# A recurrent mixture-of-experts layer on one core: subtraction of halves from GpSimd to VectorE, code bits turned four tiles at a time, and setup rearranged

## The chip, the cores and the metric

The kernel runs on 1 core of one Trainium2 chip. The metric is the device time in microseconds. A core has five engines with queues of their own: PE (TensorE, matrix products), DVE (VectorE), ACT (ScalarE), POOL (GpSimd) and SP (SyncE, which here only issues DMAs). Each works through its instructions in order, and semaphores tie them together. Sixteen DMA engines move data between HBM and the on-chip memory SBUF; PE writes its products to another on-chip memory, PSUM.

## What is computed

The input x has 16 x 1024 = 16384 tokens of 512 numbers. Cut to what matters:

```python
xn = layernorm(x)                                   # over the 512
D = fractal_dimension(xn); filt = wave_filter(D, 512)
x1 = real(ifft(fft(xn) * filt))
bits = (sigmoid(x1 @ W_el + b_el) > 0.5)            # 24 bits per token
syn = (bits @ H.T > 0.5); w = syn.sum(-1)           # a 12-bit syndrome
corrected = flip the first 12 bits where syn, if 0 < w <= 3
s = x1 + corrected @ W_le + b_le
probs = softmax(xn @ router_w.T)                    # 8 experts, the best 2 are used
out = sum over the 2: (xn @ expert[e] + prob_e) * weight_e
return x + s * silu(out)
```

## The kernel before

A tile is 128 tokens, one per partition, so there are 128 tiles. Four make a block (one load of 1 MB), eight a group (GT), and sixteen a round of routing (RT).

**First pass** (`pass_1`, line 1053). The wave filter is folded, in setup, into small matrices cs, cd and cm, so that a tile needs these steps. `total` (line 431, DVE): pp, the sum of the two halves of x, and the sum over all 512. `level` (ACT): the mean. `spread` (line 451, ACT): the sum of squares. `scale`: from it the reciprocal deviation, for half a group or a group at once. `fold` (lines 490 to 495): sd, sum and difference of the quarters of pp, on DVE, and m (mm), the difference of the halves of x, on POOL. `transpose` (line 502, PE, then line 504 on ACT): both turned, into pmt. `filt` (lines 518 to 521, PE, then line 524 on ACT): the filtered tile and the logits, py, copied to yb. `store` (SP): yb to the array yd in HBM, a block at a time. `take_ex` (line 549, DVE): 24 code logits and 8 router logits.

The main loop, from line 1068, runs g over the tiles and writes each engine's order by hand (`manual_schedule`). `total` and `spread` run up to 12 and 11 tiles ahead, `fold` two ahead, `transpose` one ahead. Loads of x are issued 17 tiles ahead into five block buffers. The eight expert matrices of 1 MB each load at tiles 6, 10, ... 34. Besides, each iteration takes one step of the bit code (`code`: `bits`, two `turn_bits`, `syndrome`, `correct`), up to four of routing (`route`), some of the lists' arithmetic (`whole_ops`, in the queue `aside`), and one scatter. `None` in such a queue ends the iteration's share.

Routing finds each token's two experts, one of 28 pairs. It makes oh, 28 columns of which one is 1 for a token, ranks tokens within a pair by matrix products over a round (`rank`), and from that their places (dst). `scatter` (line 771, POOL) writes 12 bytes per token (mean, scale, number of the token) to that pair's list in HBM. A record rec of 32 numbers per token, with the weights, the bias and the corrected bits, goes to yd. Four record buffers are used in turn.

**Second pass** (line 1380). 101 "whole" tiles hold 128 tokens of the same pair: token rows, filtered rows and records are gathered by POOL (`fetch_x`, `fetch_y`, line 1135), x is normalized (line 1189, DVE), turned (`turn`, line 1196, PE; line 1198, ACT), and multiplied with both experts (`product`, line 1228, PE, four chunks by two passes for each expert). `turn_code`, `mend` and `spread_out` add the corrected code's share. `combine` and `put` finish the row. Remaining tokens go through 61 "item" tiles of one expert each, and 27 "rest" tiles that add up two parts. AHEAD_K, AHEAD_X, AHEAD_N and AHEAD_T say how many tiles ahead the list entry, x, the normalization and the turn are done. The last group's code and the last round's routing run in the first iterations of the second pass.

Of the kernel before, what the change touches and what calls it, by code (L numbers as in the profile page):

```python
# [27 lines left out]
def pairs_of(ne=8):  # L28

    return [(a, a + d) for d in range(1, ne) for a in range(ne - d)]  # L30
# [3 lines left out]
def kernel(  # L34
# [114 lines left out]
    ht_b = p1c.tile([L, 12], BF16, name="ht_b")  # L149
# [15 lines left out]
    ht = sp.tile([L, 12], F32, name="ht")  # L165
# [23 lines left out]
    def constants():  # L189
# [26 lines left out]
        kf = kf[:, 0:KC]  # L216
# [13 lines left out]
        v.memset(eps, EPS)  # L230

    def more_constants():
# [11 lines left out]
        for r in recs:  # L244
            g.memset(r, 0.0)
            g.memset(bits_of(r)[:, :, L : L + 1], 1.0)
        for py in pys:
            v.memset(py[:, 1, X + H : WY], 0.0)

    def setup():  # L250
# [19 lines left out]
        nc.tensor.matmul(pm[:, NS - 1 :], st.own, sums[:, NS - 1 :], start=True, stop=True)  # L270
        above = sp.tile([P, NS, HW], F32, name="above")
# [7 lines left out]
        nc.tensor.matmul(pn, st.all, cnt, start=True, stop=True)  # L279
        ly = sp.tile([P, NS], F32, name="ly")  # L280
        v.tensor_scalar(ly, pn, 1.0, None, ALU.max)
        nc.scalar.activation(ly, ly, AF.Ln)
# [19 lines left out]
        v.tensor_sub(wt[:, 2:4, :], lat[:, 0:2, :], lat[:, 2:4, :])  # L302
        gain = sp.tile([P, KC], F32, name="gain")
# [10 lines left out]
        for i in range(2):  # L314
            for c in range(2):
                nc.tensor.matmul(
                    pys[1][:, i, 0:H], bas[:, 2 + c, i * P : (i + 1) * P], gbas[:, 2 + c, :],
                    start=(c == 0), stop=(c == 1),
                )
        v.tensor_add(wt[:, 0, :], wp[:, 0, :], wp[:, 1, :])  # L320
        v.tensor_sub(wt[:, 1, :], wp[:, 0, :], wp[:, 1, :])
        for g in range(2):
            total(g)
            spread(g)
        nc.scalar.copy(cs[:, X:], pys[0][:, 0, 0:Q])
        nc.scalar.copy(cd[:, X:], pys[0][:, 1, 0:Q])
        for g in range(2, 4):
            total(g)
            spread(g)
        level()  # L330
        nc.scalar.copy(cm[:, :, X:], pys[1][:, :, 0:H])
# [3 lines left out]
        fold(0)  # L335
# [12 lines left out]
        for op in scale(0, slice(0, TPT)):  # L348
            op()
# [3 lines left out]
        for g in range(4, GT):  # L353
            total(g)
            spread(g)
        level()
# [65 lines left out]
    def total(g: int):  # L422

        k, j = groups[g // GT], g % GT
        if j == 0:
            k.sum = small.tile([P, GT], F32, name="sum")
            k.sq2 = small.tile([P, GT], F32, name="sq2")
            k.low = small.tile([P, GT], F32, name="low")
# [12 lines left out]
    def level():  # L441
        while means:
            k, js = means.pop()
            nc.scalar.activation(k.low[:, js], k.sum[:, js], AF.Copy, scale=-4.0 / E)
            nc.scalar.activation(k.rec[:, js, 10], k.sum[:, js], AF.Copy, scale=1.0 / E)
# [38 lines left out]
    def fold(g: int):  # L484
# [6 lines left out]
            sd[:, 0:Q], p[:, 0:Q], k.low[:, j : j + 1], p[:, Q:H], ALU.add, ALU.add  # L491
# [3 lines left out]
        nc.gpsimd.tensor_tensor(m, xr[:, 0:H], xr[:, H:E], ALU.subtract)  # L495
# [57 lines left out]
    def code(s: int):  # L553
# [3 lines left out]
        def bits():  # L557

            k.bits = bits_of(k.rec)[:, :, 0:L]
# [4 lines left out]
        def turn_bits(h):  # L564
            if h == 0:
                k.bt = small.tile([L, GT, P], BF16, name="bt", bufs=2)
            pg = ps_g.tile([P, 512], F32, name="pg")[0:L].rearrange("l (j t) -> l j t", t=P)
            for j in range(TPT):
                nc.tensor.matmul(
                    pg[:, j, :], k.bits[:, h + j, :], ident_b, start=True, stop=True  # L570
                )
            nc.scalar.copy(k.bt[:, h : h + TPT, :], pg)

        def syndrome():
            k.pg = ps_g.tile([P, 512], F32, name="pg")[:, 0 : GT * 12].rearrange(
                "p (j n) -> p j n", n=12
            )
            for j in range(GT):
                nc.tensor.matmul(k.pg[:, j, :], k.bt[:, j, :], ht_b, start=True, stop=True)

        def correct():
# [12 lines left out]
                k.bits[:, :, 0:12], k.bits[:, :, 0:12], fix, ALU.not_equal  # L594
# [20 lines left out]
    def route(n: int):  # L615
# [30 lines left out]
        def total():  # L646
            st.sm = new("sm", [P, S])
            v.tensor_reduce(st.sm, st.pb, AX.X, ALU.add)
# [32 lines left out]
        def chosen():  # L681
            st.sel = new("sel", SN, BF16)
            v.tensor_add(st.sel, st.hot1, st.hot2)
# [7 lines left out]
        def den_of():  # L691
            st.den = new("den", [P, S])
            v.tensor_add(st.den, st.sm, st.p2)

# [3 lines left out]
            lambda: v.reciprocal(st.sm, st.sm),  # L698
            lambda: v.tensor_mul(st.p2, st.p2, st.sm),
            den_of,  # L700
            lambda: v.tensor_scalar(st.den, st.den, 1e-6, None, ALU.add),
# [4 lines left out]
        def pair(d, at):  # L706
            if d == 1:
                st.oh = new("oh", [P, S, NPAIR], BF16)
            v.tensor_mul(
                st.oh[:, :, at : at + NE - d], st.sel[:, :, 0 : NE - d], st.sel[:, :, d:NE]  # L710
            )

        at = 0
        for d in range(1, NE):
            ops.append(lambda d=d, at=at: pair(d, at))
            at += NE - d
# [3 lines left out]
        def quads():  # L720
            st.q4 = small.tile([P, 4, NPAIR], BF16, name="q4", bufs=1)[:, 0:A]
            with nc.allow_low_precision("counts up to 4"):
                v.tensor_reduce(
                    st.q4, st.oh.rearrange("p (a b) k -> p a k b", b=4), AX.X, ALU.add
                )
# [60 lines left out]
        def weigh():  # L786
            st.w1 = new("w1", [P, S])
# [746 lines left out]
```

## Time and profile before

| | |
|---|---|
| median of 3 runs | 1370.36 us (1369.69 to 1370.8) |
| the profiled execution | 1371.99 us, its span 1370.0 us |
| PE busy | 1323.9 us (97%) |
| DVE busy | 927.1 us (68%) |
| POOL busy | 884.1 us (65%) |
| ACT busy | 602.7 us (44%) |
| first eviction of a filtered tile (line 524) starts | 27.7 us |
| last one starts | 326.3 us |
| line 495, POOL, 128x256 f32 | 128 times, mean 793 ns |
| line 771, POOL, a scatter of 128 entries | 128 times, mean 1067 ns |
| line 1228, PE | 2104 matrix instructions, busy 940.0 us |

The shares are means over two very different passes, so a row has to be read in its stretch of the time. [...] The ends of PE's instructions are modelled, so distances between starts say more than durations there. ACT and DVE also begin an instruction before the one ahead has ended.

### The profile page before, as it was taken

Reading aid. Unit: us, or ns where it says so; the run is one execution under the profiler, and the core shown is the slowest. Engines: PE = TensorE matmul, PEld = TensorE weight load, DVE = VectorE, ACT = ScalarE, POOL = GpSimd, SP = SyncE. Lnnn points to the kernel's source line nnn. Section 1 sums busy time; section 2 is a strip of 40 time slices with the busy share of each in tenths; the row PEclk is TensorE's granted clock in tenths of the full one; section 3 lists DMA queues with packets and bytes.
Section 4 is the critical chain, followed back from the end, with each engine's and each line's share of the span. In section 5 each row is a group of like instructions: output and inputs, shape, how many; then the busy total and the mean of one; then the engine's idle time right before and its main releaser. Section 6 shows DMA issues by size and latency. Waiting matters only on the chain.

```text
span 1370.0 us, 18162 instructions
## 1 busy us (share of the span) xinstructions
PE 1323.9 (97%) x4944; PEld 737.5 (54%) x4944; DVE 927.1 (68%) x2635; ACT 602.7 (44%) x1298; POOL 884.1 (65%) x879
## 2 busy tenths in 40 slices
PE   5999999989999999999999999999999999999996
PEld 4887777765444444444444444444444444444442
DVE  6898999974765788611111137787778877787775
ACT  6998999975322222222222223333333333333332
POOL 3367777876767554577554046777777777777741
PEclk9999999999999999999999999999999999999998
DMA  6998877836333432355446244555555555655531
GB/s 216 353 319 283 254 243 238 256 108 201 85 104 107 141 109 76 112 170 168 138 141 190 75 134 136 181 173 179 174 172 183 179 176 175 187 173 175 181 121 39
DMA packets 119216, 233.75 MB, mean 171 GB/s; under 512 B 37356, under 2 KB 71020, under 8 KB 115023
## 3 DMA queue, kind: packets, MB, share of 16 engines
q0 software_dynamic: 47264, 135.54, 32.8%
q1 hardware_dynamic: 71386, 96.88, 21.2%
q8 instruction: 43, 0.70, 0.2%
q14 instruction: 55, 0.44, 0.1%
q10 hardware_dynamic: 468, 0.19, 0.1%
HBM read 144.79 MB, written 87.75 MB: 170 GB/s over the span
## 4 chain that ended last, share of the span: by engine, by line
PE 82%; DVE 7%; issue 4%; ACT 2%; POOL 2%; DMA 1%; POOLq 0%; DVEq 0%; SPq 0%; ACTq 0%
PE pe L1228 62%; PE py L521 5%; PE pt L1196 5%; PE pt L502 3%; PE py L518 2%; PE py L519 2%; PE pg L1261 1%; DVE pp L431 1%; DVE sd L490 1%; POOL out L1312 1%; DMA yd<-yb 1%; ACT no L451 1%; DVE sd L493 1%; ACT yb L524 1%; PE pc L1249 1%
## 5 line engine op out<-in xcount | busy, mean ns | idle before, releaser
L1228 PE MATMUL pe<-w_sb,xt 128*128 x2104 | 940.0, 594 | 1.2 <-issue 1.2
L1228 PEld LDWEIGHTS pe<-w_sb,xt 128*128 128x128 f32 x2104 | 394.9, 190 | 417.3 <-issue 411.6
L1279 ACT ACTIVATE acc<-acc,yg 128x512 f32<-128x512 f32 x128 | 92.4, 722 | 406.8 <-DVE acc L1278 406.8
L1278 DVE SCALAR_TENSOR_TENSOR acc<-pe,yg,acc 128x512 f32<-128x512 f32 x101 | 75.7, 749 | 180.2 <-PE pe L1228 180.0
L1198 ACT COPY xt<-pt 128x512 f32<-128x512 f32 x162 | 93.6, 578 | 171.7 <-PE pt L1196 171.7
L1312 POOL DMA_INDIRECT out<-xg,toks x101 | 112.3, 1112 | 82.0 <-DVE xg L1307 55.5
L771 POOL DMA_INDIRECT lists<-rec,dst x128 | 136.6, 1067 | 33.9 <-issue 22.4
L495 POOL TENSOR_TENSOR mm<-xt 128x256 f32<-128x256 f32 x128 | 101.5, 793 | 82.4 <-PE pt L502 63.5
L1189 DVE TENSOR_SCALAR xn<-xg,entry 128x512 f32<-128x512 f32 x61 | 34.8, 571 | 173.4 <-PE pt L1196 170.1
L521 PE MATMUL py<-cm,pmt 128*128 128x288 f32 x512 | 147.2, 411 | 0.0
L1135 POOL DMA_INDIRECT yg<-yd,toks x101 | 107.2, 1061 | 61.6 <-ACT acc L1279 29.6
L1135 POOL DMA_INDIRECT xg<-in_x,toks x101 | 108.6, 1075 | 40.7 <-issue 27.5
L1275 ACT ACTIVATE acc<-pe,yg 128x512 f32<-128x512 f32 x101 | 68.9, 682 | 135.0 <-PE pe L1228 102.4
L1196 PEld LDWEIGHTS pt<-ident,xn 128*128 128x128 f32 x648 | 81.0, 141 | 86.6 <-issue 84.3
L524 ACT ACTIVATE yb<-py,rec 128x640 f32<-128x640 f32 x128 | 101.5, 793 | 26.8 <-PE py L521 23.0
L1135 POOL DMA_INDIRECT xg<-in_x,entry x88 | 89.9, 1021 | 29.6 <-issue 25.9
L1135 POOL DMA_INDIRECT part<-ed,adr_r x54 | 65.7, 1217 | 65.0 <-DMA ed<-res 48.8
L521 PEld LDWEIGHTS py<-cm,pmt 128*128 128x128 f32 x512 | 91.9, 193 | 13.9
L1196 PE MATMUL pt<-ident,xn 128*128 128x128 f32 x648 | 97.3, 273 | 1.6 <-DVE xn L1189 0.8
L1307 DVE TENSOR_TENSOR xg<-mix,xg 128x512 f32<-128x512 f32 x128 | 88.5, 692 | 4.4
L451 ACT ACTIVATE no<-xt,sum 128x512 bf16<-128x512 f32 x128 | 91.0, 711 | 1.2 <-DVE pp L431 1.2
L1135 POOL DMA_INDIRECT entry<-lists,adr_i x61 | 62.9, 1032 | 41.7 <-DVE xn L1189 24.7
(270 smaller groups left out, 1766.1 us busy)
## 6 DMA issues: line engine op xcount, KB each, us to landing
xt<-in_x SPq DMA_DIRECT2D x32, 1024.0 KB
yd<-yb SPq DMA_DIRECT2D x32, 576.0 KB
yd<-yb SPq DMA_DIRECT2D x32, 512.0 KB
ed<-res SPq DMA_DIRECT2D x61, 256.0 KB
w_sb<-in_expert_w SPq DMA_DIRECT2D x8, 1024.0 KB
yd<-rec SPq DMA_DIRECT2D x36, 64.0 KB
lists<-rec,dst POOLq DMA_INDIRECT x128
xg<-in_x,toks POOLq DMA_INDIRECT x101
```

What stands on the lines that cost most here:

```text
L451: nc.scalar.activation(no, xts[g // TPT][:, g % TPT, :], AF.Square, bias=k.sum[:, j : j + 1], scale=-float(E), accum_out=k.sq2[:, j : j + 1],)
L495: nc.gpsimd.tensor_tensor(m, xr[:, 0:H], xr[:, H:E], ALU.subtract)
L521: nc.tensor.matmul(py[:, 1, 0 : X + H], pmt[:, 2 + c, :], cm[:, c, :], start=(c == 0), stop=(c == 1))
L524: nc.scalar.activation(y_room(g), py[:, :, 0:WY], AF.Copy, scale=k.rec[:, j, 11:12])
L771: dma = nc.gpsimd.indirect_dma_start(out=lists, out_offset=bass.IndirectOffsetOnAxis(ap=st.dst[:, j : j + 1], axis=0), in_=st.rec.bitcast( ...
L1135: nc.gpsimd.indirect_dma_start(out=dst, out_offset=None, in_=src, in_offset=bass.IndirectOffsetOnAxis(ap=idx, axis=0), bounds_check=limit - 1,
L1196: nc.tensor.transpose(pt[:, c * P : (c + 1) * P], k.xn[:, c * P : (c + 1) * P], ident)
L1198: nc.scalar.copy(k.xt.rearrange("p c t -> p (c t)"), pt)
L1228: nc.tensor.matmul(pe.unsqueeze(1), k.xt[:, c, :], w_sb[:, bass.ds(e, 1), c, :], start=(c == 0), stop=(c == KC - 1),)
L1279: nc.scalar.activation(k.acc, k.acc, AF.Silu, bias=k.rec[:, 9:10])
L1307: nc.vector.tensor_add(k.x, k.mix, k.x)
L1312: dma = nc.gpsimd.indirect_dma_start(out=of, out_offset=bass.IndirectOffsetOnAxis(ap=k.tok, axis=0), in_=k.x, in_offset=None, bounds_check ...
```

## The change

1. **m by VectorE.** In `fold` the difference of the halves is made by DVE. POOL has only DMA work in the pass.
2. **One mean.** `level` writes -4/512 of the sum into the record and nothing else; `fold` reads it there. Who needs the mean in the second pass multiplies by -0.25.
3. **Bits of four tiles.** The 24 bits of four tiles, now in a tile of their own, are turned by one product (96 rows), and the syndrome of four tiles comes from one product with a block-diagonal matrix. Twelve of the bits are copied to the record by ACT.
4. **Routing.** The pairs are ordered by cyclic distance, so that four products make all 28 columns; sel has 12 columns. Sums of four tiles are two additions. The two chances (probabilities) lie side by side in one tile, so that weights and biases take one operation each.
5. **Setup.** The clearing of records and of PSUM moves from POOL and from the beginning to DVE and into the setup's waits; the arguments of the filter are made behind the first products; the first tiles' sums, folds and turns are placed among the setup's steps; fewer squares (`spread`) stand ahead of the first filtered tile.
6. **The passage and the second pass.** List entry, x, normalization and turn go one tile further ahead. Turns of items use another PSUM pool; `turn_code` has four slots in one bank; `whole_ops` starts with a None, and one None more stands behind it.

The diff, cut:

```diff
 def pairs_of(ne=8):
-    return [(a, a + d) for d in range(1, ne) for a in range(ne - d)]
+    near = [(a, (a + d) % ne) for d in range(1, ne // 2) for a in range(ne)]
+    return [tuple(sorted(k)) for k in near] + [(a, a + ne // 2) for a in range(ne // 2)]
...
         for i, x_ in enumerate(lx):
             v.memset(st.slope[:, i : i + 1], -(n * x_ - sum(lx)) / den)
-        kf = kf[:, 0:KC]
+        v.memset(eps, EPS)
+        st.kf = kf[:, 0:KC]
+
+    def arguments():
+        v, kf = nc.vector, st.kf
         kr = sp.tile([P, KC], F32, name="kr")
...
-        for r in recs:
-            g.memset(r, 0.0)
-            g.memset(bits_of(r)[:, :, L : L + 1], 1.0)
-        for py in pys:
-            v.memset(py[:, 1, X + H : WY], 0.0)
+
+    def clear(r):
+        nc.vector.memset(r, 0.0)
+        nc.vector.memset(bits_of(r)[:, :, L : L + 1], 1.0)
...
         nc.tensor.matmul(pm[:, NS - 1 :], st.own, sums[:, NS - 1 :], start=True, stop=True)
+        arguments()
...
         nc.tensor.matmul(pn, st.all, cnt, start=True, stop=True)
+        clear(recs[0])
...
+        total(0)
         gain = sp.tile([P, KC], F32, name="gain")
...
+        for g in range(1, 4):
+            total(g)
         v.tensor_add(wt[:, 0, :], wp[:, 0, :], wp[:, 1, :])
         v.tensor_sub(wt[:, 1, :], wp[:, 0, :], wp[:, 1, :])
-        for g in range(2):
-            total(g)
-            spread(g)
+        spread(0)
+        level()
+        fold(0)
+        spread(1)
...
+        spread(3)
+        fold(1)
+        begin, middle, end = scale(0, slice(0, TPT))
+        begin()
         nc.scalar.copy(cs[:, 0:L], pw[:, 0, :])
         nc.scalar.copy(cd[:, 0:L], pw[:, 1, :])
         nc.scalar.copy(cm[:, :, 0:L], pw[:, 2:4, :])
-        for g in range(4, GT):
-            total(g)
-            spread(g)
-        level()
+        middle()
+        transpose(1)
+        end()
+        total(4)
+        spread(4)
+        clear(recs[1])
+        total(5)
+        spread(5)
...
-            nc.scalar.activation(k.low[:, js], k.sum[:, js], AF.Copy, scale=-4.0 / E)
-            nc.scalar.activation(k.rec[:, js, 10], k.sum[:, js], AF.Copy, scale=1.0 / E)
+            nc.scalar.activation(k.rec[:, js, 10], k.sum[:, js], AF.Copy, scale=-4.0 / E)
...
-        nc.gpsimd.tensor_tensor(m, xr[:, 0:H], xr[:, H:E], ALU.subtract)
+        nc.vector.tensor_sub(m, xr[:, 0:H], xr[:, H:E])
...
-            pg = ps_g.tile([P, 512], F32, name="pg")[0:L].rearrange("l (j t) -> l j t", t=P)
-            for j in range(TPT):
+            pg = ps_g.tile([P, 512], F32, name="pg")[0 : TPT * L, 0:P]
+            nc.tensor.matmul(
+                pg, k.bits[:, h : h + TPT, :].rearrange("p j l -> p (j l)"), ident_b, start=True, stop=True
+            )
+            nc.scalar.copy(k.bt[:, h // TPT, :], pg)
+
+        def syndrome():
+            pg = ps_g.tile([P, 512], F32, name="pg")[:, 0 : GT * 12]
+            k.pg = pg.rearrange("p (j n) -> p j n", n=12)
+            nc.scalar.copy(bits_of(k.rec)[:, :, 12:L], k.bits[:, :, 12:L])
+            for h in range(GT // TPT):
                 nc.tensor.matmul(
-                    pg[:, j, :], k.bits[:, h + j, :], ident_b, start=True, stop=True
+                    pg[:, h * TPT * 12 : (h + 1) * TPT * 12], k.bt[:, h, :], ht_b,
+                    start=True, stop=True,
                 )
...
-            st.sel = new("sel", SN, BF16)
-            v.tensor_add(st.sel, st.hot1, st.hot2)
+            st.sel = new("sel", [P, S, NE + NE // 2], BF16)
+            v.tensor_add(st.sel[:, :, 0:NE], st.hot1, st.hot2)
+            v.tensor_copy(st.sel[:, :, NE:], st.sel[:, :, 0 : NE // 2])
...
-        for d in range(1, NE):
-            ops.append(lambda d=d, at=at: pair(d, at))
-            at += NE - d
+        for d in range(1, NE // 2 + 1):
+            ops.append(lambda d=d: pair(d, (d - 1) * NE))
...
-                v.tensor_reduce(
-                    st.q4, st.oh.rearrange("p (a b) k -> p a k b", b=4), AX.X, ALU.add
-                )
+            v.tensor_add(two, o4[:, :, 0:2, :], o4[:, :, 2:4, :])
+            v.tensor_add(st.q4, two[:, :, 0, :], two[:, :, 1, :])
...
-        aside.extend([lengths, None, full, None, rows_, None, where, upto, None, bounded])
+        aside.extend([None, lengths, None, full, None, rows_, None, where, upto, None, bounded])
...
-            while spreads and spreads[0] <= g + AHEAD_S and spreads[0] <= 2 * g + GT + 4:
+            while spreads and spreads[0] <= g + AHEAD_S and spreads[0] <= 2 * g + GT - 1:
...
-    AHEAD_K, AHEAD_X, AHEAD_P, AHEAD_Y, AHEAD_N, AHEAD_T = 9, 6, 4, 5, 4, 2
+    AHEAD_K, AHEAD_X, AHEAD_P, AHEAD_Y, AHEAD_N, AHEAD_T = 10, 7, 4, 5, 5, 3
...
+    pcs = ps_c.tile([96, 4, P], F32, name="pc")
...
+        if k.kind == "item":
+            k.mean = w2.tile([P, 1], F32, name="mean1", bufs=2)
+            nc.vector.tensor_scalar(k.mean, k.low, -0.25, None, ALU.mult)
...
-        pc = ps_c.tile([96, P], F32, name="pc")
+        pc = pcs[:, k.at % 4, :]
...
+        "turn": [max(k - AHEAD_T, min(k - 2, 3)) for k in range(NTILE)],
```

## The prediction

> **What bounds the kernel now.** I first cut the span into stretches at the starts of the evictions yb<-py (line 524, one for each of the 128 tiles of the first pass). Columns: stretch, length, busy us and count of PE, PEld, DVE, ACT and POOL, granted clock, DMA share, GB/s.
>
> ```profile
> 27.70:109.00 81.30, 81.19 (x521) 65.61 (x519) 73.92 (x266) 77.14 (x185) 41.25 (x48) 1.00 0.94 320
> 109.00:120.10 11.10, 8.78 (x44) 7.04 (x45) 8.55 (x32) 8.70 (x23) 5.41 (x7) 0.85 0.97 352
> 120.10:156.10 36.00, 35.98 (x235) 28.79 (x234) 32.38 (x121) 34.73 (x84) 28.96 (x33) 1.00 0.81 250
> 156.10:194.00 37.90, 36.34 (x235) 28.89 (x234) 37.08 (x130) 35.21 (x85) 29.23 (x33) 1.00 0.75 237
> 400.00:1361.00 961.00, 957.74 (x2865) 466.53 (x2863) 597.28 (x1439) 293.22 (x575) 619.79 (x568) 1.00 0.48 149
> ```
>
> Three regimes. From 27.7 to 120 (tiles 0 to 40) the DMA engines are 94 to 97% busy, because the eight expert matrices load beside the tiles. From 120 to 326 each round of 16 tiles takes 36.0 to 43 us. From 400 PE is never idle, so the second pass can lose only what stalls at its beginning. The change can win in the start, in the five and a half rounds after 120, and in the passage at 326 to 400.
>
> Next I read the timelines inside one round: PE, then ACT.
>
> ```profile
> 121.83 0.38 PE L502 MATMUL pt<-ident,sd 128*128 128x128 f32 x2
> ...
> 123.87 0.39 PE L569 MATMUL pg<-ident_b,rec 128*24 128x128 bf16 x4
> 124.20 0.44 PE L502 MATMUL pt<-ident,sd 128*128 128x128 f32 x2
> ```
>
> ```profile
> 122.03 0.79 ACT L524 ACTIVATE yb<-py,rec 128x640 f32<-128x640 f32 x1
> ...
> 123.98 0.79 ACT L524 ACTIVATE yb<-py,rec 128x640 f32<-128x640 f32 x1
> 124.67 0.56 ACT L572 CAST bt<-pg 24x512 bf16<-24x512 f32 x1
> 125.14 0.72 ACT L451 ACTIVATE no<-xt,sum 128x512 bf16<-128x512 f32 x1
> ```
>
> A plain tile takes 1.95 us (122.03 to 123.98). PE's instructions start back to back for all of it, and so do ACT's three (starts 0.69, 0.71 and 0.55 apart): the two are tied. A tile with turn_bits takes 2.43, and the tie holds: PE adds 0.48, ACT's cast 0.47. The round at 120.1 is 16 x 1.95 = 31.2 plus 4.8 for bits, syndrome, logarithms, means and rank.
>
> The third engine, DVE, is the slowest in the later rounds (37.08 of 37.90). The timelines of POOL and DVE side by side say why:
>
> ```profile
> 122.59 0.88 POOL L495 TENSOR_TENSOR mm<-xt 128x256 f32<-128x256 f32 x1
> 123.63 0.99 POOL L771 DMA_INDIRECT lists<-rec,dst  x1 [0.16 <-issue]
> ```
>
> ```profile
> 122.34 0.34 DVE L490 SCALAR_TENSOR_TENSOR sd<-pp,low 128x128 f32<-128x128 f32 x1
> 122.60 0.28 DVE L493 TENSOR_TENSOR sd<-pp 128x128 f32<-128x128 f32 x1
> 122.81 0.95 DVE L431 SCALAR_TENSOR_TENSOR pp<-xt 128x256 f32<-128x256 f32 x1
> ```
>
> Line 431 takes 0.41 elsewhere and 0.95 beside POOL's subtraction. Over the pass, line 493 averages 503 ns where it meets line 495, 280 where it meets only a scatter, and 281 where POOL is idle. Durations above the shortest of their form, at DVE instructions that meet line 495, add up to 9.6 us in the round from tile 64. So POOL's subtraction costs DVE about 0.5 us a tile, and the scatters cost it nothing.
>
> **m moves from POOL to DVE.** The row for a 128x256 f32 operation from SBUF on DVE is in the second pass:
>
> ```profile
> 389.54 0.42 DVE L1271 TENSOR_TENSOR mix<-mix,yg 128x256 f32<-128x256 f32 x1
> ```
>
> It lasts 0.42, but independent instructions start sooner: line 431, as wide, lets its follower start 0.34 after it. I charge 0.34 (ends 0.33 and 0.46): 16 x 0.34 = 5.4 a round. [...] DVE in the worst round: busy 36.6, less 9.6 stretch, plus 5.4 (by the rule 6.8) = 32.4 (33.8).
>
> [...]
>
> **Fewer DVE instructions in routing.** Seven products of line 709 (0.19 to 0.35 each, 1.8 in all) become four of about 0.29, near line 683's 0.28: -0.6. The reduction of line 723 (0.93) becomes two additions of about 0.28: -0.4. Den's two (0.31 and 0.43) become one; weigh and biases lose one each: -0.7. The copied half of sel adds 0.2. Ends overlap, so I take -1.2 of these 1.5. DVE: 31.2 a round, below what follows.
>
> **Bits of four tiles at once.** PE: four products of line 569, 56 ns apart, become one: -0.17, four times a round. Eight of line 579 (0.28 in the chain) become two: -0.2, twice. PE: -1.1 a round. ACT: the cast of 512 columns becomes one of 128. The row with that shape, ct<-pc (line 1253), lasts 0.26, so about 0.16 of issue in place of 0.47: -1.2 a round. One mean copy of two goes: -0.4. The new copy of 12 bits per tile adds 0.13 to 0.25, twice: +0.4. ACT: -1.2. As the two are tied, only the smaller counts: 36.0 - 1.1 = 34.9 a round, so DVE's 31.2 leaves PE and ACT as the bound.
>
> Rounds: at 120.1, 36.0 to 34.9: 1.1. At 156, 37.9: 3.0. At 194, 36.9: 2.0. At 231, 37.7; this one carries the whole-list arithmetic on DVE too, so I take 35.3: 2.4. The last eight tiles: 0.6.
>
> **The stall at tile 108.** The round at 268.6 takes 43.1. POOL holds the gather tt<-lists (276.85) for its scatters to land, and m queues behind it for 3.7; then DVE waits 1.9 for tt at line 906. With m on DVE the first wait reaches no tile. The second stays and may grow to 4, since DVE gets there sooner. I take 38.5: 4.6.
>
> **Setup.** DVE reaches line 263 at 5.81 without waiting. It was held by ten operations of the arguments (3.23 to 5.71), stretched to 0.4 to 0.7 by POOL's clears. Moved behind the first products, they fill idle 1.1 between 6.27 and 7.37 and overrun it by some 0.4; the clears now on DVE (0.55 and 0.17 on POOL) fall into gaps of 0.7. The chain starts 1.9 sooner, 1.5 after the overrun. Tiles 1's fold and turn come forward too, and ACT's idle 0.7, 0.5 and 0.2 between 16.7 and 23 closes in part. Five squares (0.71 each) go behind the first eviction; it comes 6 sooner, but ACT repays 3.5 in tiles 0 to 4. Net 3.2 (ends 1.5 and 4.5). The clears of records 2 and 3 at tile 4 lie beside 1.0 of DVE idle.
>
> **Tiles 8 to 40: nothing.** The DMA engines bind. All that is issued there is the same (25 MB at 350 GB/s, my count from the issues, is 71 us). It starts with tile 6, so it is shifted by the start's 3.2 and not shortened. Faster tiles wait longer at tile 36 (now 11.7 us in the chain for yd<-yb). If that cover goes, another 2 are won.
>
> **Passage to the second pass.**
>
> ```profile
> PE pg L853 <- DVE cum L814: 2.6, 1, 2.6
> PE pe L1228 <- issue: 1.2, 1, 1.2
> ```
>
> The one None ahead of lengths puts line 853 an iteration behind cum: 2.6 gone. The granted clock was 0.5 for 3.4 us after this pause; eight products took 5.4 instead of 3.4, so 2.0 more. Next late there is scatter and gather on POOL, with no PE wait behind it. Four slots for pc save one of two round trips to ACT in three iterations, 0.3 each; the mends still wait for ct: 0.7. The seventh xg and tenth entry go ahead on POOL, 1.07 each; the first yg waits 5.2 for yd anyway, so 0 (worst +1). The turn one tile earlier and the second bank change no PE work; the added scale of the mean, one small DVE operation in 61 items and one in each kept, lies in stretches with DVE 13 to 20% busy: 0. Sum 5.2.
>
> **Sum.** 3.2 + 1.1 + 3.0 + 2.0 + 2.4 + 4.6 + 0.6 + 5.2 = 22.1. The profiled execution took 1371.99 (span 1370.0), 1.6 above the median of 1370.36; the saving is carried over: 1370.4 - 22.1 = **1348**.
>
> **The rivals.** (a) *Ties hold.* PE's and ACT's extras fall on different tiles, and DVE at 90% waits in order, so rounds stay near 36: the first five terms after the start fall to 0, 1.9, 0.9, 1.5, 3.5: sum 16.2, 1354. For it: the round now is 0.9 above PE's own sum. (b) *DMA binds on.* Share 0.75 to 0.81 would rise with the pace; if yb's two buffers then wait for stores, only start and passage remain: 8.4, 1362. Against: 40 tiles after the experts it fell to 250 GB/s from 352. (c) *Slower: DVE becomes the bound.* If the stretch is not POOL's subtraction but comes with any POOL work, DVE keeps it: 36.6 + 5.4 - 1.2 = 40.8 a round, against a mean of 38. It decides from about 38 a round on. 5.5 rounds lose some 16, less 8.4: 1378. Against it are the 280 against 281 ns. (d) The new setup order starves ACT and the start loses what the rest wins: 1370.
>
> **How the numbers follow.** Forecast 0.50, (a) 0.25, (b) 0.15, (c) 0.07, (d) 0.03. The forecast's own range is 1340 to 1354: setup 1.5 to 4.5, the tt wait 2 to 7, DMA relief. Taking in (a) and (b) gives 1338 to 1364; (c) stays out. 0.2% is 2.7 us, about what a measurement here can tell from no change. Faster 0.90, within 0.03, slower 0.07.
>
> **What would show it.** Right: line 493's successor rows at 0.28 throughout; no POOL row but DMA in the pass; rounds at 34 to 35.5 with PE and ACT full; first yb near 22; no PE wait on cum. Wrong: DVE rows still stretched; DVE over 36 in a round; tile 36 no earlier; a new half-clock stretch at the passage.

## The result and the profile after

The changed kernel takes 1347.45 us, median of 4 runs (1346.75 to 1347.89); the kernel before, beside it, 1370.03 (1368.02 to 1370.80). The ratio is 0.9832, with an interval of 0.9820 to 0.9844: **22.6 us faster**, where 22.1 were forecast. The sum came out almost right; several of its terms did not. The span of the profiled execution is 1346.1 us against 1370.0, so 23.9 us are to be found between the two traces.

The head of the page of the changed kernel, to be held against the table of before:

```profile
span 1346.1 us, 17641 instructions
...
PE 1306.1 (97%) x4752; PEld 732.5 (54%) x4752; DVE 909.7 (68%) x2802; ACT 589.1 (44%) x1282; POOL 769.1 (57%) x743
```

PE is 97% busy in both. DVE's busy time even fell, by 17 us, though it took over 128 subtractions: what it no longer spends stretched, and the shorter routing, outweigh them. POOL is 115 us less busy. None of this says where the end moved, so the pass is cut as before, at starts of yb<-py (now line 535). Columns: stretch, length, busy us and count of PE, PEld (PE's weight loads), DVE, ACT and POOL, granted clock (PE's clock as a share of full speed, so 0.5 is half clock), DMA share (busy share of the 16 DMA engines), GB/s.

```profile
21.30:104.00 82.70, 77.49 (x458) 63.92 (x456) 70.23 (x299) 77.19 (x193) 17.31 (x16) 0.98 0.91 303
104.00:119.20 15.20, 9.55 (x47) 7.33 (x48) 11.41 (x55) 8.61 (x22) 0.00 (x0) 0.78 0.83 297
119.20:153.70 34.50, 34.13 (x212) 28.41 (x211) 30.80 (x137) 33.30 (x84) 16.58 (x16) 1.00 0.93 261
153.70:188.40 34.70, 34.05 (x212) 28.32 (x211) 32.05 (x141) 33.22 (x84) 16.98 (x16) 1.00 0.95 257
258.40:292.15 33.75, 33.75 (x214) 28.42 (x212) 31.39 (x138) 30.48 (x75) 19.12 (x16) 1.00 0.59 175
```

Three things are to be seen. The rounds from 119.2 on are 34 to 35 us, with PE and ACT full and DVE at 31 to 32: the picture that was forecast. The round with the former stall (the last line) is a plain round now. But the first 40 tiles end at 119.2, though the first eviction comes 6.4 earlier than before: in the second line PE works 9.55 of 15.20 us, at a granted clock of 0.78.

The starts of yb<-py, from both traces, give the balance. The first row's 3.2 is counted at tile 8, behind the squares that ACT has to make up.

| stretch | before us | after us | won | forecast |
|---|---|---|---|---|
| to tile 8 | 43.9 | 40.7 | 3.2 | 3.2 |
| tiles 8 to 40 | 76.2 | 78.6 | -2.4 | 0 |
| round 40 to 56 | 36.0 | 34.4 | 1.6 | 1.1 |
| round 56 to 72 | 37.9 | 34.7 | 3.2 | 3.0 |
| round 72 to 88 | 36.9 | 34.2 | 2.7 | 2.0 |
| round 88 to 104 | 37.7 | 35.8 | 1.9 | 2.4 |
| round 104 to 120 (the stall) | 43.1 | 33.8 | 9.3 | 4.6 |
| last eight tiles | 14.6 | 13.4 | 1.2 | 0.6 |
| from the last eviction to the end | 1043.7 | 1040.5 | 3.2 | 5.2 |

**DVE.** Its costliest groups from 115 to 260 us in the changed kernel: line, names, shapes and count, then busy us and mean ns of one.

```profile
L443 DVE SCALAR_TENSOR_TENSOR pp<-xt 128x256 f32<-128x256 f32 x66 | 27.7, 420 | 0.0
L506 DVE TENSOR_TENSOR mm<-xt 128x256 f32<-128x256 f32 x66 | 27.6, 418 | 0.0
...
L504 DVE TENSOR_TENSOR sd<-pp 128x128 f32<-128x128 f32 x67 | 19.1, 286 | 0.0
```

The same lines in the kernel before, from 150 to 275 us:

```profile
L431 DVE SCALAR_TENSOR_TENSOR pp<-xt 128x256 f32<-128x256 f32 x54 | 25.4, 470 | 0.0
L493 DVE TENSOR_TENSOR sd<-pp 128x128 f32<-128x128 f32 x54 | 19.4, 360 | 0.0
```

The subtraction (line 506) lasts 418 ns, as long as the second pass's row of that width in the trace of before (0.42 us); line 504, the old line 493, is at 286 on average, where it was 360 over all its instances there, 503 over those beside POOL's subtraction. POOL's scatters still run, and stretch nothing: over the whole first pass line 504 is at 286 in the 58 instances that meet a scatter, at 284 in the 70 others.

**The wait at tile 36.** ACT's timeline, the eviction of that tile; in brackets is the idle time before it, and what ended it:

```profile
108.30 0.79 ACT L535 ACTIVATE yb<-py,rec 128x640 f32<-128x640 f32 x1 [6.65 <-DMA yd<-yb]
```

The buffer yb is still being stored. The chain of work that ended last says how long the store of tiles 28 to 31, whose buffer tile 36 needs, held it up: start and length, first before, then now.

```profile
97.19 11.71 DMA yd<-yb
```

```profile
93.38 14.81 DMA yd<-yb
```

From tile 35 to tile 36 it is now 8.9 us, before 5.3, and the granted clock is 0.5 for 6.8 us from 106.8, before for 3.4 from 112.6. This is where the -2.4 of the table sits.

**The pause for tt.** POOL's timeline, then DVE's one line that reads the gathered tt:

```profile
248.06 0.97 POOL L787 DMA_INDIRECT lists<-rec,dst  x1 [0.30 <-issue]
256.62 1.25 POOL L907 DMA_INDIRECT tt<-lists,idx  x1 [7.58 <-DVE sd L504]
262.81 3.07 POOL L787 DMA_INDIRECT lists<-rec,dst  x1 [4.94 <-DVE woff L905]
```

```profile
264.90 0.32 DVE L918 COPY ttf<-tt 30x256 f32<-30x256 f32 x1
```

The same two in the kernel before:

```profile
276.85 1.06 POOL L895 DMA_INDIRECT tt<-lists,idx  x1 [3.74 <-DVE ex L549]
```

```profile
281.23 0.32 DVE L906 COPY ttf<-tt 30x256 f32<-30x256 f32 x1 [1.88 <-DMA tt<-lists,idx]
```

POOL has finished a round's scatters by 249, tt is issued at 256.62, 1.7 us ahead of the eviction of tile 104, and DVE reaches it 8.3 us later. Before, it was issued 8.3 us behind that eviction (268.56), and read 4.4 later. There is no idle time before line 918: DVE's wait for tt went wholly, not in part.

**The passage.** PE's instructions that waited for an engine's result, in three stretches from 305 to 347 us:

```profile
307.32 0.66 PE L1222 MATMUL pt<-ident,xn 128*128 128x128 f32 x4 [1.77 <-DVE xn L1211]
308.70 1.11 PE L1222 MATMUL pt<-ident,xn 128*128 128x128 f32 x4 [0.72 <-ACT xt L1224]
...
334.97 0.22 PE L1275 MATMUL pc<-ident_b,b 128*96 128x128 bf16 x1 [0.92 <-ACT ct L1279]
345.51 0.66 PE L1222 MATMUL pt<-ident,xn 128*128 128x128 f32 x4 [0.86 <-ACT xt L1224]
347.00 0.22 PE L1275 MATMUL pc<-ident_b,b 128*96 128x128 bf16 x1 [0.78 <-ACT ct L1279]
```

The wait for cum (2.6) is gone, with the half-clock stretch behind it. But the second pc product still waits for ACT's ct, as it did before by the same 0.92, though it now writes another slot: the slots saved nothing. Two turns fall into one iteration and wait for ACT's copy, a wait of 0.86 that was not there. And a half-clock stretch at 308 lasts 6.8 us, where the one at 331 in the trace of before lasted 3.4. So the time at half clock behind the last eviction is 6.8 in both traces (before 3.4 at 331 and 3.4 behind cum). Of the 3.2 won there, 1.5 is PE's idle time (21.0 to 19.4) and 1.7 its busy time, with twelve instructions fewer.

### The profile page after: what moved, and what is told of

Read it like the earlier page. It is cut to its first block, busy times and chain, and to the rows that moved or that the text cites. A ratio compares the mean times of both kernels' runs of the same rounds, so it can differ in the third digit from the quotient of the medians.

```text
span 1346.1 us, 17641 instructions
## 1 busy us (share of the span) xinstructions
PE 1306.1 (97%) x4752; PEld 732.5 (54%) x4752; DVE 909.7 (68%) x2802; ACT 589.1 (44%) x1282; POOL 769.1 (57%) x743
## 4 chain that ended last, share of the span: by engine, by line
PE 84%; ACT 5%; issue 4%; DMA 3%; POOL 1%; DVE 1%; POOLq 0%; SPq 0%; ACTq 0%; DVEq 0%
PE pe L1254 63%; PE py L532 6%; PE pt L1222 3%; DMA yd<-yb 3%; PE pt L513 3%; PE py L529 2%; PE pg L1222 2%; ACT no L462 2%; PE py L530 2%; PE pg L1287 1%; ACT yb L535 1%; ACT pmt L515 1%; POOL out L1338 1%; PE pc L1275 1%; DMA xt<-in_x 0%
## 5 line engine op out<-in xcount | busy, mean ns | idle before, releaser
L1338 POOL DMA_INDIRECT out<-xg,toks x101 | 108.6, 1075 | 82.9 <-DVE xg L1333 56.7
L1211 DVE TENSOR_SCALAR xn<-xg,mean,entry 128x512 f32<-128x512 f32 x61 | 34.7, 569 | 166.7 <-PE pg L1222 166.3
L1224 ACT COPY xt<-pg 128x512 f32<-128x512 f32 x56 | 32.8, 586 | 156.7 <-PE pg L1222 156.7
L1154 POOL DMA_INDIRECT part<-ed,adr_r x54 | 62.8, 1163 | 64.9 <-DMA ed<-res 48.8
L1332 DVE TENSOR_TENSOR mix<-mix,acc 128x512 f32<-128x512 f32 x128 | 87.6, 685 | 0.8 <-ACT acc L1305 0.8
L1222 PEld LDWEIGHTS pt<-ident,xn 128*128 128x128 f32 x424 | 53.2, 142 | 58.5 <-issue 51.1
L515 ACT COPY pmt<-pt 128x512 f32<-128x512 f32 x128 | 73.7, 576 | 1.8 <-PE pt L513 1.6
```

Source lines behind the costliest of these rows:

```text
L515: nc.scalar.copy(pmts[g], pt)
L1154: nc.gpsimd.indirect_dma_start(out=dst, out_offset=None, in_=src, in_offset=bass.IndirectOffsetOnAxis(ap=idx, axis=0), bounds_check=limit - 1,
L1222: nc.tensor.transpose(pt[:, c * P : (c + 1) * P], k.xn[:, c * P : (c + 1) * P], ident)
L1332: nc.vector.tensor_mul(k.mix, k.mix, k.acc)
L1338: dma = nc.gpsimd.indirect_dma_start(out=of, out_offset=bass.IndirectOffsetOnAxis(ap=k.tok, axis=0), in_=k.x, in_offset=None, bounds_check ...
```

## The experiments

The runs met chips of two kinds. Most fell on chips where the kernel before takes 1370 to 1372 us, as above. On two others it takes 1444.2 and 1458.5 us, and there the parts of the change behave differently; apart from the run on the bits, the runs of those chips are told last. The theory under test is the prediction's: POOL's subtraction stretches DVE, and once it is gone PE and ACT set the pace.

### The subtraction back on POOL, all else changed

```diff
-        nc.vector.tensor_sub(m, xr[:, 0:H], xr[:, H:E])
+        nc.gpsimd.tensor_tensor(m, xr[:, 0:H], xr[:, H:E], ALU.subtract)
```

> The changed kernel with m back on POOL once more, since the first time the kernel before itself took 1444. If the chip gives before near 1370 again: theory (POOL's subtraction stretches DVE and ties POOL to the loop) 1360 to 1365 with rounds after tile 40 at 36 to 37 and the tt wait back; rival (the stretch only fills idle DVE) 1347 to 1351. If before is near 1444 again: about 1428 as the first time.

Measured: 1369.97 us (1366.15 to 1371.64) beside 1371.97, ratio 0.9984 (0.9974 to 0.9994). That is above the 1360 to 1365 expected: everything else together is worth 2 us without this one line. The groups of DVE from 130 to 260 us:

```profile
L443 DVE SCALAR_TENSOR_TENSOR pp<-xt 128x256 f32<-128x256 f32 x54 | 26.0, 481 | 0.0
L504 DVE TENSOR_TENSOR sd<-pp 128x128 f32<-128x128 f32 x53 | 25.4, 480 | 0.0
```

and one round of it, in the columns of the stretches above:

```profile
152.80:190.90 38.10, 35.21 (x211) 28.10 (x209) 37.14 (x124) 34.00 (x83) 29.62 (x32) 1.00 0.81 236
```

Line 504 is back at 480 ns, with fewer DVE instructions than before, and the round is DVE's: 37.14 busy of 38.10. Three rounds (56 to 104) take 38.1, 38.1 and 38.8, where 36 to 37 were expected, and the round with tt 45.1. So PE's and ACT's savings had nothing to win.

### The kernel before with only the subtraction moved

```diff
-        nc.gpsimd.tensor_tensor(m, xr[:, 0:H], xr[:, H:E], ALU.subtract)
+        nc.vector.tensor_sub(m, xr[:, 0:H], xr[:, H:E])
```

> The kernel before with m on DVE alone, once more. On a chip that gives before near 1371: theory (m's move carries nearly all of the gain, since with m on POOL the other parts gave 2 us): -12 to -17, so 1354 to 1359, rounds after tile 40 at 36.0 to 36.5 (PE and ACT tied, bits as before), no pause at tile 108. Rival (DVE needs the shorter routing as well: 32.4 a round is not enough slack in order): rounds at 37 and more, -3 to -8. Rival (m's move is worth nothing without the new setup and bits): within 3 us of before.

Measured: 1365.74 us (1363.79 to 1368.62) beside 1370.46, ratio 0.9969 (0.9958 to 0.9979): 4.7 faster, where more than twice that was expected. Groups of DVE from 130 to 260 us, then two rounds:

```profile
L495 DVE TENSOR_TENSOR mm<-xt 128x256 f32<-128x256 f32 x57 | 23.8, 417 | 0.0
...
L493 DVE TENSOR_TENSOR sd<-pp 128x128 f32<-128x128 f32 x57 | 16.3, 286 | 0.0
```

```profile
120.30:156.33 36.03, 36.02 (x235) 28.83 (x234) 31.85 (x137) 34.76 (x85) 16.38 (x16) 1.00 0.88 258
156.33:192.36 36.03, 36.02 (x235) 28.82 (x234) 33.05 (x144) 34.76 (x85) 17.05 (x16) 1.00 0.91 248
```

In the pass the theory held: DVE is unstretched, and the plain rounds are 36.03 and 36.03, PE busy 36.02, with the old bits. The pause for tt is gone here too. From the first to the last eviction 9.7 us are won (298.6 to 288.9). The passage and second pass gave 1.4 back (1045.1), and the profiled execution was the fastest of the eight, 1.9 below their median. So the size for the whole kernel was missed, the mechanism was not.

The two runs together: one part alone is worth 4.7, all the others alone 2.0, both 22.6. Two bounds lay close above each other, DVE at 37 to 38 a round and PE with ACT at 36; lifting either shows the other.

### Bits turned one tile at a time

```diff
-            pg = ps_g.tile([P, 512], F32, name="pg")[0 : TPT * L, 0:P]
-            nc.tensor.matmul(
-                pg, k.bits[:, h : h + TPT, :].rearrange("p j l -> p (j l)"), ident_b, start=True, stop=True
-            )
+            pg = ps_g.tile([P, 512], F32, name="pg")[0:L].rearrange("l (j t) -> l j t", t=P)
+            for j in range(TPT):
+                nc.tensor.matmul(
+                    pg[:, j, :], k.bits[:, h + j, :], ident_b, start=True, stop=True
+                )
...
-            for h in range(GT // TPT):
+            for j in range(GT):
                 nc.tensor.matmul(
...
+                    k.pg[:, j, :], k.bt[:, j, :], ht_b[0:L, 0:12], start=True, stop=True
                 )
```

> The changed kernel with the bits turned, and the syndromes made, tile by tile as before, all else as changed. Theory (PE and ACT are tied once DVE is free, so each turn costs 0.4 to 0.5 a tile again): rounds after tile 40 longer by 1.1 to 1.6 (a tile with a turn 2.43 and 2.5 in place of 2.02 and 2.11), 5.4 rounds, +6 to +8, so 1353 to 1356. Rival (another engine binds, the turns are covered): rounds within 0.4, +0 to +2.

This ran on the chip where the kernel before takes 1458.5, beside the changed kernel without the None ahead of lengths (told below): 1546.96 (ratio 1.0657, 1.0575 to 1.0740) against 1530.66. Both stall there behind tile 27, so the 16 us between them are not used. Tiles 8 to 24 are undisturbed in both: 35.7 us against 34.2, so the bits are worth 1.5 us a round, within the 1.1 to 1.6 expected. What that makes of the whole kernel on the other chips was not measured. PE's timeline says where, first with bits one by one, then four at once:

```profile
43.70 0.39 PE L581 MATMUL pg<-ident_b,bits 128*24 128x128 bf16 x4
44.03 0.44 PE L513 MATMUL pt<-ident,sd 128*128 128x128 f32 x2
```

```profile
44.64 0.22 PE L580 MATMUL pg<-ident_b,bits 128*96 128x128 bf16 x1
44.69 0.39 PE L513 MATMUL pt<-ident,sd 128*128 128x128 f32 x2
```

From the first turn of bits to PE's next instruction it is 0.33 us, then 0.05: 0.28 saved, four times a round. The same reading of the syndrome gives 0.28 and 0.05: 0.23, twice. That sums to 1.6, where the prediction had 1.1.

### POOL tied to the loop by something that costs DVE nothing

A copy of one number of the previous tile's yb on POOL ahead of each scatter, so that POOL cannot run ahead.

```diff
+                if scatters:
+                    nc.gpsimd.tensor_copy(pace[0:1, :], ybs[(g - 1) // TPT][0:1, (g - 1) % TPT, 0, 0:1])
                 throw(1)
```

> The changed kernel with one copy of a single number on POOL ahead of each scatter, which waits for the eviction of the tile before, so that POOL goes with the loop. Theory (POOL let loose issues 16 scatters in 20 us, beside the record stores, and that piles up at tile 36; but it also has the gather tt issued early): the wait at tile 36 falls from 8.9 to 3 to 5, tile 40 at 114 to 116; the pause for tt at tile 107 comes back with 4 to 9; total within 4 of 1347.5, no DVE row over 0.2 longer than without. Rival (the pace of POOL means nothing): both places as in the changed kernel, total the same to 1 us. Rival (any POOL instruction that reads SBUF stretches DVE by 0.5): rounds at 36 and more, +10 and more.

Measured: 1351.39 us (1350.78 to 1353.38) beside 1370.46, ratio 0.9866 (0.9849 to 0.9882), 3.9 slower than the changed kernel. Line 504 is at 284 ns, so DVE is not stretched. The pause for tt is back:

```profile
264.90 0.98 POOL L907 DMA_INDIRECT tt<-lists,idx  x1 [3.96 <-ACT pmt L515]
```

```profile
268.79 0.32 DVE L918 COPY ttf<-tt 30x256 f32<-30x256 f32 x1 [5.91 <-DMA tt<-lists,idx]
```

tt is issued 8.3 us later than in the changed kernel (8.5 behind the eviction of tile 104, nearly as in the kernel before), DVE waits 5.91 for it, and the round takes 39.1 in place of 33.8. At the same time tile 40 comes 1.5 earlier (117.75). These two make 3.8 between them; the spans of the two traces differ by 2.9. So the pause came from POOL's being tied to the loop, by whatever it waited for. The other half of the theory did worse: the step to tile 36 fell only from 8.9 to 7.5, where 3 to 5 were expected.

### The expert matrices twelve tiles apart

To tell whether the wait at tile 36 is a matter of where the eight loads fall:

```diff
-            if g >= 4 and g % TPT == 2 and g // TPT <= NE:
-                load_expert(g // TPT - 1)
+            if g % 12 == 6 and g // 12 < NE:
+                load_expert(g // 12)
```

> The changed kernel with expert loads every 12 tiles once more. If the chip gives before near 1370: theory (expert loads saturate the DMA engines to tile 40 and take back the start's gain) tile 40 at about 110 in place of 119, total 1338 to 1341; rival (the loss only moves) within 3 of 1347. If before is near 1444 again: about 1507 as the first time, the stalls then come with the chip and with scatters that POOL issues back to back.

Measured: 1360.17 us (1359.53 to 1364.90) beside 1371.97, ratio 0.9926 (0.9905 to 0.9947): worse than the changed kernel. SP's queue, then ACT's timeline:

```profile
121.82 1.47 SPq L545 DMA_DIRECT2D yd<-yb  x2
123.40 5.32 SPq L624 DMA_DIRECT2D yd<-rec  x4
```

```profile
102.84 0.79 ACT L535 ACTIVATE yb<-py,rec 128x640 f32<-128x640 f32 x1 [3.04 <-DMA yd<-yb]
...
143.49 0.79 ACT L535 ACTIVATE yb<-py,rec 128x640 f32<-128x640 f32 x1 [3.71 <-DMA yd<-yb]
...
182.16 0.80 ACT L535 ACTIVATE yb<-py,rec 128x640 f32<-128x640 f32 x1 [1.58 <-DMA yd<-yb]
```

The wait at 36 is shorter (5.27 between the evictions), but others come at tiles 52, 68, 84 and 100 (3.3 to 8.0), behind the record stores (line 624) of each round. With a DMA share of 0.93 in a plain round of the changed kernel, there was no room left in which these matrices loaded unseen. The loss moved, as the rival had it, and it grew: tile 40 comes at 115.0, not at the theory's 110, and the total is 12.7 above the changed kernel's, where the rival allowed 3.

### The expert matrices early

```diff
-            if g >= 4 and g % TPT == 2 and g // TPT <= NE:
-                load_expert(g // TPT - 1)
+            if g == 0:
+                for e in range(3):
+                    load_expert(e)
+            if g >= 4 and g % TPT == 2 and g // TPT <= NE - 3:
+                load_expert(g // TPT + 2)
```

> The changed kernel with three expert loads at tile 0, where the DMA engines are 13 to 63% busy, and the other five at tiles 6 to 22. Theory (the wait at tile 36 pays off all DMA work that has piled up until then): 9 us of loads lie in the idle stretch, the wait falls from 8.9 to 1 to 4, tile 40 is evicted at 111 to 114 in place of 119.2, total 1340 to 1343. Rival (the record stores and the scatters issued back to back make the wait by themselves, whatever has been loaded): the wait stays over 6 us and the total within 3 of 1347.5.

Measured: **1340.00 us** (1338.47 to 1341.38) beside 1370.46, ratio 0.9781 (0.9765 to 0.9798): it beats both kernels. The stretch from tile 32 to tile 40, first of the changed kernel, then of this one:

```profile
93.47:119.24 25.77, 18.68 (x102) 14.55 (x101) 17.32 (x79) 16.82 (x43) 6.95 (x7) 0.87 0.93 291
```

```profile
91.63:110.09 18.46, 17.64 (x111) 14.54 (x110) 17.67 (x82) 16.84 (x44) 8.04 (x8) 1.00 0.96 279
```

With nearly the same work on every engine, 25.77 become 18.46, and the clock of 0.87 becomes 1.00. The step from tile 35 to 36 falls from 8.88 to 2.84; tile 40 starts 9.2 earlier, and 9.4 arrive at the end of the span (7.5 between the medians of the two kernels, taken beside different runs of the kernel before). The store that held up tile 36 now stands in the chain with

```profile
91.06 9.36 DMA yd<-yb
```

in place of 14.81; no matrix is issued in the 10 us ahead of it, where in the changed kernel one went out 1.8 us ahead. So the wait at tile 36 is mostly DMA work that piled up ahead of that store, and loading during the first tiles, when the DMA engines are 13 to 63% busy (from 20 to 35 us in the changed kernel), takes it off.

The same edit in the kernel before:

> The kernel before with three expert loads at tile 0 and five at tiles 6 to 22. Theory (the wait at tile 36 pays for piled-up DMA work in both kernels): its 5.3 gap falls to 2.5 to 3.5 and the half-clock stretch behind it goes, tile 40 at 115.5 to 117 in place of 120.1, total 1365.5 to 1367; the difference to the changed kernel with the same loads at tile 40 is then the start's 3.2 and the rounds' 1.2 each. Rival (the wait is the changed kernel's alone): within 1.5 of before.

It ran on the chip of 1458.5: 1454.50 (1444.24 to 1458.70), ratio 0.9988 (0.9951 to 1.0025), no difference that can be told there. In its trace tile 36 comes without a wait (2.53 after tile 35), and tile 40 at 116.2, as expected; but on this chip a single stall of 19.8 us follows in the passage, and the total cannot say what the edit is worth elsewhere.

### The chips on which the kernel before takes 1444 and 1458

The first four runs fell on the first of these. Three of them are edits shown above.

> The changed kernel with m back on POOL, all else as changed. Theory (POOL's subtraction stretches DVE by about 0.5 us a tile, and ties POOL to the loop): DVE rows beside it at 0.5 and more, rounds after tile 40 at 36 to 37 in place of 34.2 to 35.8, the wait for tt near tile 108 back with 4 to 6 us; in all +12 to +18, so 1360 to 1365. Rival (the gain of the rounds comes from the fewer PE and ACT instructions, the stretch fills idle DVE): rounds within 0.5 of the changed kernel's, +0 to +4, so 1347 to 1351.

The subtraction back on POOL: 1428.15 (1414.32 to 1435.89) beside 1444.20, ratio 0.9851 (0.9736 to 0.9965).

> The kernel before with m on DVE alone. Theory: DVE falls from 36.6 to about 32.4 a round and PE and ACT bind at 36.0, so the rounds at 156, 194 and 231 lose 1.9, 0.9 and 1.5, and the pause near tile 108 goes (5 to 6 us), since POOL no longer waits with the loop: -8 to -12, so 1358 to 1362. Rival (stretch comes with any POOL work): DVE at 41 a round, rounds at 41, +10 to +20. Rival (all parts are needed together): within 3 us of 1370.

The kernel before with the subtraction on DVE: 1523.34, ratio 1.0589 (1.0496 to 1.0681), the opposite sign of the same edit on the other chips.

> The changed kernel with the eight expert loads every 12 tiles (tiles 6 to 90) in place of every 4 (6 to 34). Theory (the expert loads saturate the DMA engines up to tile 40 and take back what the start won): the 8.9 us wait at tile 36 goes, tile 40 is evicted at about 110 in place of 119.2, later rounds lose at most 1 each to DMA: -6 to -9, so 1338 to 1341. Rival (x loads and yb stores bind by themselves, or the start's gain is lost elsewhere): tile 40 within 2 us of 119, or the loss moves to the later rounds, and the total is within 3 of 1347.

The matrices twelve tiles apart: 1507.51, ratio 1.0456 (1.0367 to 1.0544).

> The changed kernel without the None ahead of lengths (and five instead of six behind it). Theory as predicted: PE waits 2.6 us for cum in the passage again and runs 3.4 us more at half clock, 2.0: +4 to +5, so 1351.5 to 1352.5; nothing changes near tile 108. Rival (DVE has cum ready, or the time of the half clock does not depend on this wait): no wait over 1 us on cum, or a wait without a further half-clock stretch: +0 to +2.6.

The None ahead of lengths taken out, to put PE's product on cum back next to its sum:

```diff
-        aside.extend([None, lengths, None, full, None, rows_, None, where, upto, None, bounded])
+        aside.extend([lengths, None, full, None, rows_, None, where, upto, None, bounded])
...
-    routes += route(len(rounds) - 1) + [lambda: whole_ops(1)] + [None] * 6
+    routes += route(len(rounds) - 1) + [lambda: whole_ops(1)] + [None] * 5
```

1507.36, ratio 1.0471 (1.0367 to 1.0576). It ran again, on the chip of 1458.5:

> The changed kernel without the None ahead of lengths, once more. On a chip that gives before near 1371: theory as predicted: PE waits 2.6 for cum in the passage and a half-clock stretch follows, +3.5 to +5, so 1351 to 1352.5. Rival (the changed kernel's own half-clock stretch at the start of the passage is as long, so that only the wait counts, or less): +0 to +2.6.

1530.66, ratio 1.0548 (1.0469 to 1.0628). The totals say nothing of what the None is worth, but the traces do. PE's product on cum, without the None, then in the changed kernel:

```profile
461.53 0.23 PE L865 MATMUL pg<-ones_b,cum 128*28 128x128 bf16 x1 [3.56 <-DVE cum L826]
```

```profile
366.09 0.23 PE L865 MATMUL pg<-ones_b,cum 128*28 128x128 bf16 x1
```

Without it PE waits 3.56 for cum, in both runs, and the clock is then 0.5 for some 3.4 us; with it there is neither. So the theory's mechanism held; the gain in time on the other chips stays unmeasured. The changed kernel itself did not run on these chips; this run is the nearest to it, and its trace shows a loss of another kind. POOL's timeline, first and last scatter of a round, then ACT's:

```profile
126.72 1.13 POOL L787 DMA_INDIRECT lists<-rec,dst  x1 [24.88 <-ACT pmt L515]
...
146.58 0.97 POOL L787 DMA_INDIRECT lists<-rec,dst  x1 [0.30 <-issue]
```

```profile
145.56 0.79 ACT L535 ACTIVATE yb<-py,rec 128x640 f32<-128x640 f32 x1 [6.27 <-remote]
149.81 0.59 ACT L515 COPY pmt<-pt 128x512 f32<-128x512 f32 x1 [2.75 <-remote]
```

POOL, free of the loop, issues a round's 16 scatters back to back, 1.28 apart. While it does, ACT, DVE and PE stand idle for several us at a time, mostly with no releaser that the profile can name ("remote"). Tiles 40 to 48 take 31.2 us here, 16.4 in the changed kernel. The eight tiles after the burst are nearly as quick as there (18.6 against 18.0). The kernel before with early matrices, on the same chip, shows the same link in the passage, where POOL issues gathers and scatters back to back. POOL's last issue there, then ACT, then PE:

```profile
371.19 1.06 POOL L1138 DMA_INDIRECT xg<-in_x,toks  x1 [0.30 <-issue]
```

```profile
372.52 0.59 ACT L1201 COPY xt<-pt 128x512 f32<-128x512 f32 x1 [5.76 <-remote]
```

```profile
374.88 0.26 PE L1252 MATMUL pc<-ident_b,b 128*96 128x128 bf16 x1 [19.76 <-ACT ct L1256]
```

The stall ends when POOL's issue does. On the other chips the same bursts stand beside full speed. The kernels with the subtraction on POOL, which ties it to the loop, lose nothing of this kind in the first pass; those with it on DVE lose 4.6 to 6.6% on these chips. Behind the first pass all lose: from the last eviction to the end the kernel with the subtraction back on POOL takes 1102 us here and 1040 on the other chips, the one without the None 1139 where the changed kernel takes 1041. What differs between the chips is open, and that pacing the scatters would help there was not tried.

## Why the prediction was right, and where not

- **"m moves from POOL to DVE": right.** The stretch belonged to POOL's subtraction and not to its scatters: 286 ns in the changed kernel and in the kernel before with that one line moved, 480 with it put back. DVE was forecast at 31.2 a round and is busy 30.8 to 32.1 in plain rounds. The rival that DVE becomes the bound fell here.
- **"Fewer DVE instructions in routing": not seen in the end.** With the old routing DVE has 31.9 to 33.1 a round, also below PE's 36.02. The saving bought slack only, as far as these runs show; none had the new bits with the old routing. The 6.8 a round in brackets for the move of m, and the 33.8 with it, are shown by no run: line 506 lasts 418 ns, but DVE's next instruction starts 335 ns after it (median of 123), 5.4 a round, as charged.
- **"Bits of four tiles at once": right, the term too small.** The "-1.1 a round" was 1.5, by what the four products cost PE, 0.28 and not 0.17; the prediction's own lines had 0.33 from the first of them (123.87) to PE's next instruction (124.20), and it counted three steps of 56 ns. The 1.5 explains most of the first round's 1.6. The rival "ties hold", in which rounds stay near 36, fell: it is what the kernel shows with the old bits.
- **"The stall at tile 108": the direction right, the size half.** The prediction let DVE's wait for tt "stay" and "grow to 4", because DVE would arrive sooner. It overlooked that POOL, having no subtraction to wait with, issues tt sooner too: 1.7 us ahead of the eviction of tile 104, where before it was 8.3 behind it. Tied to the loop again, POOL brought the pause back; free, the round wins 9.3 in place of 4.6.
- **"Setup": right, the exact hit by luck.** 3.2 at tile 8. The first eviction came 6.4 sooner, and ACT took 3.2 of it back. The prediction had 6 and 3.5, which make 2.5 and not its 3.2.
- **"Tiles 8 to 40: nothing": this step failed.** The DMA work was to be "shifted by the start's 3.2 and not shortened", so that the 3.2 would last. At tile 40 only 0.8 was left. The DMA engines' work did not simply shift: in the changed kernel they moved 303 GB/s up to 104 us, before 320 up to 109, and the store in the way of tile 36 took 14.8 us in place of 11.7, with a longer half-clock stretch behind it. With the subtraction on POOL the shift did hold: tile 40 at 116.13, 3.9 earlier than before. Of the 3.1 between that and the changed kernel's 119.24, pacing the scatters gave back 1.5; the rest is not settled. That loading earlier wins 9.2 at tile 40 shows how large the reserve in this cover was; the prediction put it at 2. One of its signs of being wrong, "tile 36 no earlier", came nearly true: tile 36 is 0.7 earlier.
- **"Passage": 3.2 in place of 5.2** (its parts make 5.3). The wait for cum and the half clock behind it went, as said. "Four slots for pc", 0.7, gave nothing: the products still wait for ct. All four slots lie in one tile of the program and in the same 96 partitions; no run tried them apart, so why the second product still waits for ct is not shown. "The turn one tile earlier ... 0" was an omission: 0.86 at 345.5. The half-clock stretch at 308 of 6.8 in place of 3.4 takes back what was won behind cum; with the early loads, where it lasts 3.4, PE is busy 1.0 less from the last eviction to the end (1020.0 against 1021.1). This was the sign "a new half-clock stretch at the passage", come half true.
- **"DMA binds on": its premise came true, its end did not.** The share in a round rose from 0.81 to 0.93, and yet plain rounds keep their pace. Adding loads to such rounds, with the matrices twelve tiles apart, brought waits of 3.3 to 8.0 between evictions.

That 22.1 came so near to 22.6 is thus in part luck, errors that cancel: about 6.2 too little at tt, rounds and the last tiles, 4.4 too much at tiles 8 to 40 and in the passage.

## What to carry to other kernels

Where two bounds lie a few per cent apart, ask of each part of a change what it is worth with the other bound in place: here 2.0 and 4.7 apart, 22.6 together. POOL, taken out of the loop, did not only stop waiting: it ran ahead. The gather tt was issued 1.7 us ahead of the eviction of tile 104 in place of 8.3 behind it, and the first pass's scatters 1.28 us apart (median) in place of 2.13. Both reached tiles that the change does not touch: the round with tt won 9.3 us, and with the scatters paced tile 40 came 1.5 earlier. A wait at the end of a loading phase was here a debt, and the time to pay it lay in the first tiles, when the DMA engines were 13 to 63% busy.

## What was unexpected of the hardware

- One edit, one line, is worth -0.3% on the chips where the kernel before takes 1370 us and +5.9% on one where it takes 1444. The stalls fall into stretches in which POOL issues indirect DMAs about 1.3 us apart. The cause is open.
- A one-element copy on POOL that reads SBUF before each scatter left DVE's line 504 at 284 ns; the 128x256 subtraction there made it 480. The stretch goes with POOL's wide operation; a short access of POOL (the copy lasts 0.18 to 0.48 us) does not show it.
- Three short PE gaps (1.77, 0.72 and 0.62 us) went with 6.8 us at a clock of 0.5, where gaps of 1.81, 0.72 and 1.12 in the kernel with early loads went with 3.4. What decides the length was not settled.
